# Attention's matrix in the middle of a one-core kernel: VectorE's order fixed, strided sums as trees, and v's products ahead

## The chip, the cores and the metric

The kernel runs on one core of a Trainium2 chip. The metric is the device time of one execution in microseconds (us): the median of three runs before the change is 2695.53 us (2695.43 to 2703.38). A core has a matrix engine (TensorE, here PE), a vector engine (VectorE, DVE), a scalar engine with function tables (ScalarE, ACT), a general engine (GpSimd, POOL) and a queue engine (SyncE, SP). Each takes its own instructions in order and waits on the others through semaphores. DMAs are issued from SP's, ACT's and POOL's queues.

## The reference

The input is `x`, 1 x 384 x 192 x 192, float32. Layer 0 is a preactivated attention over channels, layer 1 a depthwise 7x7 convolution; each is added to its input after a group norm with 32 groups.

```python
qkv = einsum('bchw,oc->bohw', gn(x), w_qkv) + b_qkv      # 1152 channels
qkv = qkv.reshape(b, 3*c, 96, 2, 96, 2).max(axis=(3, 5)) # 2x2 max pool
qkv = depthwise3x3(qkv, w_dw) + b_dw
q, k, v = split(qkv)                                     # 8 heads of 48 channels, 9216 pixels
q, k = q / norm(q), k / norm(k)
attn = einsum('bhcn,bhdn->bhcd', q, k) * temperature     # 8 matrices of 48 x 48
out = sum(topk_softmax(attn, kk) @ v * a for kk, a in zip((24, 32, 36, 38), (a1, a2, a3, a4)))
out = repeat2x2(gelu(out))
x = x + einsum('bchw,oc->bohw', out, w_proj) + b_proj
x = x + depthwise7x7(gn(x), symmetrized(w7))
```

`topk_softmax` keeps the kk largest of the 48 entries of a row and takes the softmax over them.

## The kernel before

The 384 channels lie as three tiles of 128 partitions (`KT = 3`). The kernel has four stages, one after the other on the chip:

1. Statistics of the first group norm, with the weights scaled by them.
2. q and k: products, pooling and nine taps of the depthwise convolution for 24 bands of rows; the squares for the norms; transposes; and `grams`, the 96 x 96 products of pairs of heads, summed in PSUM over all bands (`products`). Towards its end v's first two row blocks are convolved in between (`xvb`).
3. v: a loop over 16 blocks of rows. Block `i` takes part in this way: `load_v(i, t0)` loads a third of it (`t0` = 0, UT, 2 UT) on SP's queue into one of three slots of `xvs`; `convolve(i, t0, ct, ...)` makes six matmuls into a tile of the PSUM pool `pv`, which has **two** buffers, and pools it on VectorE with one reduce (line 569) into the tile `rows`; `depthwise_v(i, ct, dys)` makes three taps on VectorE for each `dy`, into `vb`; `attend(i)` multiplies `vb` by `attnT` (tile `po`) and takes Gelu on ScalarE; `project` multiplies by the projection (tile `pr`, copied out as `y`); `residual` adds `x` on VectorE (tile `sx`), sums squares on ScalarE and stores by POOL's queue. Its four adds per channel tile are counted below as residual adds. Loop turn `i` attends `j = i - 2`, so at its start blocks up to 2 must have been convolved in full.
4. The 7x7 convolution as matmuls (line 1909), with the weights laid out as band matrices.

Between stages 2 and 3 stands the function `attention`, a generator that is advanced in steps (`yield`) while v's products are issued around it. It scales `grams` by the norms of k (`scaled`), gathers the heads' 48 x 48 pieces with ten small DMAs into `att` (128 partitions x 3 x 48), multiplies by q's norms, and then finds each entry's rank in its row by comparing it with all others. The row's two halves of 24 are compared with each other (`sq`, 24 x 24) and within themselves (`tri`, 2 x 24 x 24, cut by the triangle `lower`); sums along both directions of these squares give `seconds`, `firsts`, `before` and `behind`. The rank decides, for each of the four kk, which of the exponentials `ex` stay (`em`); they are normalized, weighted and added to `mix`. `mix` goes by ten small DMAs into the block matrix `diag`, which seven PE transposes (tile `aT`) turn into `attnT`.

Two things set the order on an engine. A tile framework inserts the semaphores that the data need and lets a scheduler choose the order; an instruction passed through `keep` (`tc.keep_in_program_order`) stays in the order in which the program issues it, among those that are kept. Before the change `attention`'s VectorE instructions are not kept: the scheduler mixes them with v's taps and poolings. Attention runs while blocks 2 and the first third of block 3 are convolved, and block 1's taps (for attend(1), the loop's first) are made beside it.

Of the kernel before, what the change touches and what calls it, by code (L numbers as in the profile page):

```python
# [86 lines left out]
def conv_preact_d2(  # L87
# [468 lines left out]
    def convolve(i, t0, ct, xb, pin):  # L556
        b, rows = order[i], place(i)
        o = (2 * KT + ct) * P
        ps = pv.tile([P, UT, 512], F32, name=f"pv{b}_{t0}_{ct}", tag="pv")
        for u in range(UT):  # L560
            for kt in range(KT):
                pin(
                    nc.tensor.matmul(  # L563
                        ps[:, u, 0 : RB * HW], wq[:, kt, o : o + P], xb[:, u, kt, :],
                        start=(kt == 0), stop=(kt == KT - 1),
                    )
                )
        pin(
            nc.vector.tensor_reduce(  # L569
                rows[ct][:, 1 + t0 : 1 + t0 + UT, 1 : PS + 1],  # L570
                ps[:, :, 0 : RB * HW].rearrange("p u (a w b) -> p u w a b", a=2, b=2),
                AX.XY,
                ALU.max,
            )
        )

    with ExitStack() as bx:
# [628 lines left out]
        for _ in products(NB - 1, sides.pop(NB - 1)):  # L1206
            pass
        for args in xvb:
            convolve(*args, pe_keep)
        for tiles in vrows:  # L1210
            row_borders(tiles)
# [3 lines left out]
    def attention(ap):  # L1215

        HH = HC // 2
        lower = ap.tile([P, HH, HH], F32, name="lower")
        nc.gpsimd.memset(lower, 1.0)
        nc.gpsimd.affine_select(  # L1220
            out=lower, in_=lower, compare_op=ALU.is_gt, fill=0.0, base=0,
            pattern=[[1, HH], [-1, HH]], channel_multiplier=0,
        )
# [3 lines left out]
        for i, (mt, r0, r1, h) in enumerate(PIECES):  # L1227
# [3 lines left out]
        scores = nc.vector.tensor_tensor(  # L1231
            att, att, rn[:, 0:KT].unsqueeze(2).to_broadcast([P, KT, HC]), ALU.mult
        )
        yield

        rank = ap.tile([P, KT, HC], F32, name="rank")
        after = ap.tile([P, HH], F32, name="after")
        with tc.issue_after(scores.ins):  # L1240
            nc.vector.tensor_reduce(after, lower.rearrange("p d e -> p e d"), AX.X, ALU.add)
# [3 lines left out]
        for mt in range(KT):  # L1245

            full = [P, HH, HH]
            sq = ap.tile(full, F32, name=f"sq{mt}", tag="sq")
            nc.vector.tensor_tensor(
                sq,  # L1250
                att[:, mt, 0:HH].unsqueeze(1).to_broadcast(full),
                att[:, mt, HH:].unsqueeze(2).to_broadcast(full),
                ALU.is_ge,
            )
            yield
            nc.vector.tensor_reduce(seconds[:, mt], sq, AX.X, ALU.add)
            nc.vector.tensor_reduce(
                firsts[:, mt], sq.rearrange("p d e -> p e d"), AX.X, ALU.add
            )
            yield  # L1260

            full = [P, 2, HH, HH]
            halves = att[:, mt, :].rearrange("p (s d) -> p s d", s=2)
            tri = ap.tile(full, F32, name=f"tri{mt}", tag="tri")
            nc.vector.tensor_tensor(
                tri, halves.unsqueeze(2).to_broadcast(full),
                halves.unsqueeze(3).to_broadcast(full), ALU.is_ge,
            )
            yield
            nc.vector.tensor_tensor(  # L1270
                tri, tri, lower.unsqueeze(1).to_broadcast(full), ALU.mult
            )
            yield
            for t, order in ((before, "p s d e -> p s d e"), (behind, "p s d e -> p s e d")):
                nc.vector.tensor_reduce(
                    t[:, mt].rearrange("p (s d) -> p s d", s=2), tri.rearrange(order), AX.X,
                    ALU.add,
                )
                yield
        nc.vector.tensor_tensor(rank, before, behind, ALU.subtract)  # L1280
        halves = rank.rearrange("p t (s d) -> p (t s) d", s=2)
        nc.vector.tensor_tensor(
            halves, halves, after.unsqueeze(1).to_broadcast([P, 2 * KT, HH]), ALU.add
        )
        nc.vector.tensor_tensor(rank[:, :, HH:], rank[:, :, HH:], seconds, ALU.add)
        nc.vector.scalar_tensor_tensor(
            rank[:, :, 0:HH], rank[:, :, 0:HH], float(HH), firsts, ALU.add, ALU.subtract
# [3 lines left out]
        row3 = [P, KT, HC]  # L1291
        top = ap.tile([P, KT], F32, name="top")
        nc.vector.tensor_reduce(top, att, AX.X, ALU.max)
        ex = ap.tile(row3, F32, name="ex")
        nc.vector.tensor_tensor(ex, att, top.unsqueeze(2).to_broadcast(row3), ALU.subtract)
        nc.scalar.activation(ex, ex, AF.Exp)
        yield
        mix = ap.tile(row3, F32, name="mix")
        for i, kk in enumerate(KKS):
            em = ap.tile(row3, F32, name=f"em{i}", tag="em")  # L1300
            nc.vector.scalar_tensor_tensor(em, rank, float(kk), ex, ALU.is_lt, ALU.mult)
            rs = ap.tile([P, KT], F32, name=f"rs{i}", tag="rs")
            nc.vector.tensor_reduce(rs, em, AX.X, ALU.add)
            nc.vector.reciprocal(rs, rs)
            nc.vector.tensor_scalar_mul(rs, rs, aw[:, i : i + 1])
            rsb = rs.unsqueeze(2).to_broadcast(row3)
            if i == 0:
                nc.vector.tensor_tensor(mix, em, rsb, ALU.mult)
            else:
                nc.vector.tensor_tensor(em, em, rsb, ALU.mult)  # L1310
                nc.vector.tensor_tensor(mix, mix, em, ALU.add)
            yield
        diag = ap.tile([P, KT, C], F32, name="diag")
        nc.gpsimd.memset(diag, 0.0)
        for i, (mt, r0, r1, h) in enumerate(PIECES):
            eng = (nc.gpsimd, nc.scalar)[i % 2]
            eng.dma_start(diag[r0:r1, mt, h * HC : (h + 1) * HC], mix[r0:r1, mt, :])
        yield "last"
        for dt in range(KT):
# [9 lines left out]
            for l, h in ((lo, min(hi, TURN)), (max(lo, TURN), hi)):  # L1329
                if l < h:  # L1330
                    o = (l - TURN) % C
                    nc.vector.tensor_copy(attnT[:, dt, o : o + h - l], ps[:, l:h])
# [23 lines left out]
    vbs, begun = {}, set()  # L1356

    def depthwise_v(i, ct, dys, pin=lambda ins: ins):

        b = order[i % NBC]  # L1360
        if (i, ct) not in vbs:
            tag = f"vlast{i}" if i >= NBC - 1 else "vb"
            vbs[i, ct] = vp.tile(
                [P, NT, PS], F32, name=f"vb{i}_{ct}", tag=tag, bufs=KT if i >= NBC - 1 else 2 * KT
            )
        dst = vbs[i, ct]
        for dy in dys:
            r = b + dy - 1
            t0 = 1 + r // NBC
            rows = place(i + dy - 1)[ct]  # L1370
            for j in range(3):
                src = rows[:, t0 : t0 + NT, j : j + PS]
                w = wd[:, 2 * KT + ct, 3 * dy + j : 3 * dy + j + 1]
                if (i, ct) in begun:
                    pin(nc.vector.scalar_tensor_tensor(dst, src, w, dst, ALU.mult, ALU.add))  # L1375
                else:
                    begun.add((i, ct))
                    pin(
                        nc.vector.tensor_scalar(
                            dst, src, w, bdb[:, 2 * KT + ct : 2 * KT + ct + 1], ALU.mult, ALU.add  # L1380
                        )
                    )


    AHEAD = 3
    with tc.tile_pool(name="ap", bufs=1) as ap:
        chain, seen = attention(ap), []

        def advance(n):
            for _ in range(n):  # L1390
                if "last" not in seen:
                    seen.append(next(chain))

        advance(9)
        i = AHEAD - 1
        for t0 in range(0, NT, UT):
            xb = load_v(i, t0)
            with tc.issue_after(multiplied):
                for ct in range(KT):
                    convolve(i, t0, ct, xb, lambda ins: ins)  # L1400
            advance(6)
        for ct in range(KT):
            depthwise_v(1, ct, (0, 1))

        advance(99)
        xb = load_v(AHEAD, 0)
        for ct in range(KT):
            depthwise_v(AHEAD - 2, ct, (2,), keep)
            convolve(AHEAD, 0, ct, xb, keep)
        for _ in chain:  # L1410
            pass

    bpm = const.tile([P, KT], F32, name="bpm")
    with tc.issue_after(settled):
        nc.vector.tensor_tensor(bpm, bp, mean0, ALU.subtract)
    ysum = const.tile([P, KT, NBC, 2], F32, name="ysum")
# [146 lines left out]
    for i in range(AHEAD, NBC):  # L1563
# [7 lines left out]
        xb = load_v(i, UT)  # L1571
        for ct in range(KT):
            depthwise_v(i - 1, ct, (0, 1), keep)
            if ct == 1:
                convolve(i, UT, 0, xb, keep)
        convolve(i, UT, 1, xb, keep)
        if spare[i - AHEAD]:
            depthwise_v(*spare[i - AHEAD][:2], spare[i - AHEAD][2:], keep)
        convolve(i, UT, 2, xb, keep)
# [425 lines left out]
```

## Time and profile before

| what | value |
|---|---|
| median of three runs | 2695.53 us |
| the profiled execution, and its span | 2711.91 us, 2710.2 us |
| busy: PE, DVE, ACT, POOL | 93%, 84%, 52%, 54% of the span |
| last `grams` matmul ends | 1311.2 us |
| `scaled`, `att` x rn, last `mix` start | 1311.40, 1320.10, 1383.06 us |
| first `po` of attend(1), attend(2), attend(3) | 1392.07, 1443.21, 1492.60 us |
| mean granted clock of PE | 0.982 |

Times are microseconds from the start of the span. In the profile's rows an instruction is named by engine, line, operation and tiles; "[2.08 <-DMA xv]" behind a row is the idle time of that engine before it and what ended it. A row with "x5" merges five instructions in a row, and its time is from the first's start to the last's end. Every fp32 matmul shows as two records. Where engines are put side by side, `(x189)` is a count of instructions, PEclk the granted clock as a share of full speed, and the DMA share the mean of the 16 DMA engines. Waits are given as total us, times, and the longest.

### The profile page before, as it was taken

Reading aid. Unit: us, or ns where it says so; the run is one execution under the profiler, and the core shown is the slowest. Engines: PE = TensorE matmul, PEld = TensorE weight load, DVE = VectorE, ACT = ScalarE, POOL = GpSimd, SP = SyncE. Lnnn points to the kernel's source line nnn. Section 1 sums busy time; section 2 is a strip of 40 time slices with the busy share of each in tenths; the row PEclk is TensorE's granted clock in tenths of the full one; section 3 lists DMA queues with packets and bytes.
Section 4 is the critical chain, followed back from the end, with each engine's and each line's share of the span. In section 5 each row is a group of like instructions: output and inputs, shape, how many; then the busy total and the mean of one; then the engine's idle time right before and its main releaser. Section 6 shows DMA issues by size and latency. Waiting matters only on the chain. (4 is left out here: it accounts for less than half of the span.)

```text
span 2710.2 us, 29562 instructions
## 1 busy us (share of the span) xinstructions
PE 2512.9 (93%) x8893; PEld 1632.4 (60%) x8893; DVE 2268.1 (84%) x3161; ACT 1419.6 (52%) x2710; POOL 1462.8 (54%) x1588
## 2 busy tenths in 40 slices
PE   0298999999999999999889989999999799999998
PEld 0144565656666656555556646666667577777776
DVE  7986788888888888888689969898888789888987
ACT  0032667676767676775112223223225577777776
POOL 1013788888887988875112311001001578787886
PEclk9999999999999999999999989999999899999999
DMA  9962354445453545433429996756747999999998
GB/s 378 394 245 53 117 163 135 137 139 165 131 169 102 175 128 170 128 98 76 136 80 331 372 316 210 250 195 221 239 143 246 331 347 367 371 372 367 372 368 263
DMA packets 467582, 609.59 MB, mean 225 GB/s; under 512 B 250160, under 2 KB 399264, under 8 KB 450656
## 3 DMA queue, kind: packets, MB, share of 16 engines
q1 hardware_dynamic: 406928, 311.80, 36.9%
q0 software_dynamic: 37376, 148.85, 15.4%
q10 hardware_dynamic: 23120, 147.07, 14.4%
q8 instruction: 71, 1.16, 0.2%
q14 instruction: 87, 0.71, 0.1%
HBM read 370.93 MB, written 208.21 MB: 214 GB/s over the span
## 5 line engine op out<-in xcount | busy, mean ns | idle before, releaser
L563 PE MATMUL pv<-xv,wq 128*128 128x384 f32 x1512 | 502.7, 493 | 27.2 <-DMA xv<-in_x_dram 13.5
L1909 PE MATMUL pc<-main,w 128*128 128x288 f32 x1536 | 435.2, 406 | 3.6 <-issue 2.2
L563 PEld LDWEIGHTS pv<-xv,wq 128*128 128x128 f32 x1512 | 290.8, 193 | 230.9 <-DVE rows L569 16.3
L1929 DVE TENSOR_SCALAR apart<-pc,rb 32x576 f32<-32x576 f32 x384 | 312.2, 813 | 75.9 <-PE pc L1909 51.8
L869 POOL TENSOR_TENSOR qk<-qk,more 128x384 f32<-128x384 f32 x290 | 309.6, 1074 | 110.2 <-ACT more L868 101.3
L1927 ACT ACTIVATE apart<-pc,rb 32x576 f32<-32x576 f32 x384 | 281.1, 732 | 133.2 <-PE pc L1909 128.4
L1543 POOL DMA_DIRECT2D sd<-sx x96 | 72.2, 755 | 507.4 <-DVE sx L1502 486.9
L1909 PEld LDWEIGHTS pc<-main,w 128*128 128x128 f32 x1536 | 289.8, 189 | 87.8 <-issue 3.2
L1375 DVE SCALAR_TENSOR_TENSOR vb<-rows,wd,vb 128x576 f32<-128x576 f32 x384 | 312.5, 816 | 10.8
L869 POOL TENSOR_TENSOR qk<-qk,rows 128x384 f32<-128x384 f32 x216 | 230.3, 1070 | 76.3 <-ACT rows L868 70.1
L1909 PE MATMUL pc<-aux,h 128*128 128x288 f32 x768 | 248.5, 406 | 0.5 <-issue 0.3
L901 DVE SCALAR_TENSOR_TENSOR bank_r<-ring,wd,bank_r 128x384 f32<-128x384 f32 x383 | 236.1, 617 | 6.9
L1868 POOL COPY res<-apart 128x1152 f32<-128x1152 f32 (+1 forms) x96 | 224.1, 2360 | 11.1 <-ACT apart L1927 7.3
L1009 PE MATMUL bank_b<-rows,more 128*128 128x384 f32 x528 | 220.4, 499 | 1.9 <-ACT bank_c L1111 0.9
L1502 DVE TENSOR_TENSOR sx<-xr,y 128x576 f32<-128x576 f32 x180 | 203.5, 1172 | 20.7 <-ACT y L1473 14.9
L569 DVE TENSOR_REDUCE rows<-pv 128x192 f32<-128x768 f32 x144 | 137.5, 955 | 69.7 <-PE pv L563 69.6
L1522 ACT ACTIVATE wq<-sx,negmid 128x1152 f32<-128x1152 f32 x96 | 120.6, 1256 | 114.5 <-DVE sx L1502 110.2
L1089 DVE TENSOR_TENSOR rows<-bank_c,rows 128x384 f32<-128x384 f32 x132 | 73.2, 555 | 127.3 <-PE bank_c L1009 69.0
L1752 DVE SCALAR_TENSOR_TENSOR w<-eye,sb,w 128x512 f32<-128x512 f32 x96 | 174.5, 1857 | 1.5
L1909 PEld LDWEIGHTS pc<-aux,h 128*128 128x128 f32 x768 | 144.9, 189 | 42.7 <-POOL main L1817 2.0
L868 ACT ACTIVATE more<-ring,wd 128x384 f32<-128x384 f32 x290 | 170.3, 608 | 0.0
L1009 PE MATMUL bank_x<-xq,wq 128*128 128x384 f32 x378 | 154.7, 491 | 1.0 <-ACT bank_b L1061 1.0
(342 smaller groups left out, 4803.9 us busy)
## 6 DMA issues: line engine op xcount, KB each, us to landing
sd<-sx POOLq DMA_DIRECT2D x96, 600.0 KB, 10.1
out_dram<-res SPq DMA_DIRECT2D x192, 288.0 KB, 10.7
main<-sd ACTq DMA_DIRECT2D x46, 1200.0 KB, 6.3
xr<-in_x_dram SPq DMA_DIRECT2D x45, 1152.0 KB, 12.8
xq<-in_x_dram SPq DMA_DIRECT2D x21, 2304.0 KB, 8.4
xv<-in_x_dram SPq DMA_DIRECT2D x126, 384.0 KB, 7.4
w<-wt ACTq DMA_DIRECT2D x46, 1024.0 KB, 7.5
xs<-in_x_dram SPq DMA_DIRECT2D x24, 1536.0 KB, 15.2
```

Source lines behind the costliest of these rows:

```text
L563: nc.tensor.matmul(ps[:, u, 0 : RB * HW], wq[:, kt, o : o + P], xb[:, u, kt, :], start=(kt == 0), stop=(kt == KT - 1),)
L868: keep(nc.scalar.mul(part.rearrange("p (h w) -> p h w", w=PS), src, w))
L869: keep(nc.gpsimd.tensor_tensor(flat, flat, part, ALU.add))
L901: nc.vector.scalar_tensor_tensor(into, src, w, before, ALU.mult, ALU.add)
L1009: nc.tensor.matmul(ps[:, 0:HN], lhs, rhs, start=start, stop=True, skip_group_check=True)
L1375: pin(nc.vector.scalar_tensor_tensor(dst, src, w, dst, ALU.mult, ALU.add))
L1502: nc.vector.tensor_tensor(bass.AP(flat.tensor, flat.offset + at(e) + a * RUN, [flat.ap[0], [JP, NT], [1, NJ], [at(f) - at(e), 2]],), xq[:, ...
L1752: nc.vector.scalar_tensor_tensor(mid, eye.unsqueeze(1).to_broadcast([P, 4, P]), sb[:, c : c + 1], mid, ALU.mult, ALU.add,)
L1868: keep(copy(res[ps, k], apart[ps, :, k].rearrange("p e n -> p n e")))
L1909: nc.tensor.matmul(ahead[q][:, k, 0 : NT * NJ], lhs, rhs, start=(j == 0), stop=(j == 2), skip_group_check=True,)
L1927: keep(nc.scalar.mul(dst, src, scale))
L1929: keep(nc.vector.tensor_scalar_mul(dst, src, scale))
```

## The change

In words, in the order of the program:

- `depthwise_v` moves up in the file, unchanged. Block 1's first taps, `dy` = 0, for all three channel tiles (nine taps), are issued right after the last `products` and before the last of `xvb`, and those of `dy` = 1 for tile 0 (three taps) after it; all are kept in order. Their sums lie in a tile `vb_early` in the space of the weights' tile `g`.
- In `attention` every VectorE instruction of the chain but `scaled` and `after` is kept. `lower` is made after `att`'s DMAs on POOL, and its sum `after` is issued before the scores.
- The sums along the strided direction, `firsts` and `behind`, are no longer reduces but five adds of halves each (`halved`).
- The top and the exponentials are issued ahead of the rank's sums, followed by a Gelu on one element.
- The four kk's exponentials lie in one array `em`, so that one reduce, one reciprocal and one multiplication serve all four.
- `diag`'s ten DMAs go over three queues, SP's among them, instead of two.
- The middle third of block 3 (`load_v(3, UT)` and its three `convolve`s) moves from loop turn 3, between attend(1) and its `project`, to before attend(1). The seven transposes stand before the last of them. Block 1's other taps of `dy` = 1 and those of `dy` = 2 are each issued in front of one of block 3's six convolutions.

As built, nothing else changes its place but a few instructions of loop turn 3: PE has the transposes between the fifth and sixth convolution of block 3, and `project` directly behind attend(1); VectorE has tile 1's residual adds among block 2's last taps.

```diff
+        early = gwp.tile([P, GR * GQ * TR], F32, name="vb_early", tag="g")
+        for ct in range(KT):
+            vbs[1, ct] = early[:, ct * PBC : (ct + 1) * PBC].rearrange("p (t c) -> p t c", c=PS)
+        for tiles in vrows[0:2]:
+            row_borders(tiles)
+        for ct in range(KT):
+            depthwise_v(1, ct, (0,), keep)
         for args in xvb:
             convolve(*args, pe_keep)
-        for tiles in vrows:
-            row_borders(tiles)
+        depthwise_v(1, 0, (1,), keep)
+        row_borders(vrows[2])
...
-        lower = ap.tile([P, HH, HH], F32, name="lower")
-        nc.gpsimd.memset(lower, 1.0)
...
+        tt = lambda *args: keep(nc.vector.tensor_tensor(*args))
+        total_of = lambda dst, src: keep(nc.vector.tensor_reduce(dst, src, AX.X, ALU.add))
...
+        def halved(dst, t):
+
+            for n in (HH // 2, HH // 4, HH // 8):
+                tt(t[:, :, 0:n], t[:, :, 0:n], t[:, :, n : 2 * n], ALU.add)
+            tt(t[:, :, 0], t[:, :, 0], t[:, :, 1], ALU.add)
+            tt(dst, t[:, :, 0], t[:, :, 2], ALU.add)
...
-            nc.vector.tensor_reduce(seconds[:, mt], sq, AX.X, ALU.add)
-            nc.vector.tensor_reduce(
-                firsts[:, mt], sq.rearrange("p d e -> p e d"), AX.X, ALU.add
-            )
+            total_of(seconds[:, mt], sq)
+            halved(firsts[:, mt].unsqueeze(1), sq.unsqueeze(1))
             yield
...
+            total_of(before[:, mt].rearrange(by_half, s=2), tri)
+            halved(behind[:, mt].rearrange(by_half, s=2), tri)
+            yield
...
+        ready_to = ap.tile([P, 1], F32, name="ready_to")
+        keep(nc.scalar.activation(ready_to, halfneg[:, 0:1], AF.Gelu))
...
+        for i, kk in enumerate(KKS):
+            keep(
+                nc.vector.scalar_tensor_tensor(em[:, i], rank, float(kk), ex, ALU.is_lt, ALU.mult)
+            )
+        total_of(rs.rearrange("p i t -> p (i t)"), em.rearrange("p i t c -> p (i t) c"))
+        keep(nc.vector.reciprocal(rs, rs))
...
-            eng = (nc.gpsimd, nc.scalar)[i % 2]
+            eng = (nc.gpsimd, nc.scalar, nc.sync)[i % 3]
             eng.dma_start(diag[r0:r1, mt, h * HC : (h + 1) * HC], mix[r0:r1, mt, :])
...
+        for t0 in range(0, NT, UT):
+            xb = load_v(i, t0)
+            for ct in range(KT):
+                next(chain)
+                convolve(i, t0, ct, xb, keep)
+        xb = load_v(AHEAD, 0)
+        next(chain)
+        assert next(chain) == "last"
+        for ct in range(KT):
+            if ct > 0:
+                depthwise_v(1, ct, (1,), keep)
+            convolve(AHEAD, 0, ct, xb, keep)
+        xb = load_v(AHEAD, UT)
+        for ct in range(KT):
+            if ct == KT - 1:
+                for _ in chain:
+                    pass
+            depthwise_v(AHEAD - 2, ct, (2,), keep)
+            convolve(AHEAD, UT, ct, xb, keep)
...
-        xb = load_v(i, UT)
+        if i > AHEAD:
+            xb = load_v(i, UT)
         for ct in range(KT):
             depthwise_v(i - 1, ct, (0, 1), keep)
-            if ct == 1:
+            if ct == 1 and i > AHEAD:
                 convolve(i, UT, 0, xb, keep)
```

## The prediction

> **What bounds the kernel now.** I read the engine table and the 40 slices first: PE is busy 93% of the span, at 9 tenths in nearly every slice. The chain that ended last covers only the last 10 us, so it says nothing of the middle. So I looked for the stretch in which the change lives, where PE is not full, with busy time by stretch:
>
> ```profile
> core 0: us, PE busy (x) PEld busy (x) DVE busy (x) ACT busy (x) POOL busy (x), PEclk, DMA share, GB/s
> 1311.20:1392.07 80.87, 64.71 (x189) 36.45 (x188) 72.04 (x103) 5.79 (x22) 9.64 (x15) 0.92 0.43 140
> 1392.07:1443.21 51.14, 51.14 (x168) 33.05 (x169) 41.80 (x59) 15.05 (x31) 15.76 (x17) 0.97 0.52 185
> ...
> 1443.00:1492.00 49.00, 49.00 (x169) 31.71 (x168) 44.65 (x51) 13.77 (x30) 11.87 (x16) 1.00 0.94 317
> ```
>
> The first row is the attention stage: from the end of the last `grams` matmul to the first `po` matmul of attend(1). PE idles 80.87 - 64.71 = 16.2 us, at clock 0.92. The second is block 3 of the loop (attend(2) ends it), the third a later block: both full. After 1443 the loop is PE-bound, with one hole of 13.5 us at 1568-1585 (PE on DMA `xv`), and the last stage is 99% PE again. So I count up to the first matmul of attend(2), 1443.21 in this execution: what moves that moves the end. What PE waits for in the stage, by the waits, then VectorE's timeline:
>
> ```profile
> PE pv L563 <- DVE rows L569: 16.1, 6, 7.2
> ...
> 1311.40 0.55 DVE L1225 TENSOR_TENSOR scaled<-grams,rkb 96x384 f32<-96x384 f32 x1 [2.08 <-DMA xv<-in_x_dram]
> 1315.30 0.96 DVE L569 TENSOR_REDUCE rows<-pv 128x192 f32<-128x768 f32 x1 [3.35 <-PE pv L563]
> 1320.10 0.31 DVE L1231 TENSOR_TENSOR att<-att,rn 128x144 f32<-128x144 f32 x1 [3.84 <-DMA att<-scaled]
> ...
> 1331.48 3.00 DVE L1275 TENSOR_REDUCE behind<-tri 128x48 f32<-128x1152 f32 x1
> 1334.39 1.57 DVE L1257 TENSOR_REDUCE firsts<-sq 128x24 f32<-128x576 f32 x1
> ...
> 1383.06 0.29 DVE L1311 TENSOR_TENSOR mix<-mix,em 128x144 f32<-128x144 f32 x1
> 1383.28 3.72 DVE L1375 SCALAR_TENSOR_TENSOR vb<-rows,wd,vb 128x576 f32<-128x576 f32 x5
> ...
> 1394.53 4.24 DVE L1375 SCALAR_TENSOR_TENSOR vb<-rows,wd,vb 128x576 f32<-128x576 f32 x5
> 1403.73 0.96 DVE L569 TENSOR_REDUCE rows<-pv 128x192 f32<-128x768 f32 x1 [4.96 <-PE pv L563]
> ```
>
> PE waits for VectorE's pooling (L569): `pv` has two buffers, and the reduce that frees one stands in VectorE's queue behind attention's matrix. From 1320 to 1383 VectorE never rests but for 1.45 us. Of PE's own timeline I need these:
>
> ```profile
> 1311.20 11.80 PE L563 MATMUL pv<-xv_begun,wq 128*128 128x384 f32 x36
> 1336.89 22.16 PE L563 MATMUL pv<-xv,wq 128*128 128x384 f32 x60 [4.31 <-DVE rows L569]
> 1383.19 5.72 PE L563 MATMUL pv<-xv,wq 128*128 128x384 f32 x12 [7.21 <-DVE rows L569]
> 1388.75 0.93 PE L1325 MATMUL aT<-ident,diag 128*128 128x128 f32 x7
> 1392.07 7.75 PE L1441 MATMUL po<-vb,attnT 128*128 128x288 f32 x24 [2.39 <-DVE attnT L1332]
> ```
>
> Twelve records are one convolution: 3.92 us at full clock (11.77 for 36, at 1399.65). After a hole of over 2 us PE is slow for a while: 60 records took 22.16 instead of 19.6 (2.5 lost), 12 took 5.72 (1.8), 24 of `po` 7.75 instead of 5.98 (1.8).
>
> **What one link costs on VectorE.** In the five taps at 1383.28 neighbours belong to different sums: (3.72 - 0.81)/4 = 0.73 apart, that is duration less 0.085. In the five at 1394.53 each needs the one before: (4.24 - 0.81)/4 = 0.86, duration plus 0.04. Here a rule speaks. The Trainium skill, "VectorE: DVE Perf Modes", section "The DRAIN you can't avoid", says that the next operation starts only when the pipe has emptied and that a semaphore costs nothing extra. By it, fixing the order costs nothing. By these rows each dependent neighbour costs 0.125 more, and the new order, built, has 99 instructions that wait on VectorE itself between `scaled` and attend(2): 12 us if all were free before, perhaps half of it new, since the scheduler had interleaved sums. I take the rows.
>
> **Part 1, twelve taps in front.** Nine stand between `rkb` (ends 1309.3) and `scaled`: 3 x (0.57 + 2 x 0.81 + links) = 6.7 us or so, so `scaled` ends at 1316.3 instead of 1311.95. 2.1 us of it lies in the wait for `grams`, the rest delays the scores by 4.4. The other three come among the matrix's work. All twelve, about 10 us, leave the end of the stage.
>
> **Part 2, copies and `lower`.** `scaled`'s end to `att` took 8.15 us (1311.95 to 1320.10). POOL's five DMAs now stand before the memset and the select (0.58 and 0.84 us), which held the first back to 1313.80; ACT's five have no fill among them. `scaled` to landing: four issues of 0.61, then 4.3 median, 6.7. Floor 5.9 (five issues of 0.525, memset, select, then the reduce `after`, 1.57); ceiling 8.15. I take 6.7: `att` at 1323.0, 2.9 later than before. The 1.57 of `after` leaves the chain for this wait.
>
> **Part 3, the matrix.** Per third: sq 0.75, seconds 0.75, sq's tree, tri 1.35, times lower 1.35, before 1.35, tri's tree. Tree sizes 288, 24 and 48 have no row; between rows at 72 (0.22), 144 (0.30) and 576 (0.75) elements 288 comes to 0.45, and 24 to 0.17. The same page, on its errata, gives fp32 adds (N + 151)/0.96 ns: 457 and 182. sq's tree: 0.45 + 0.30 + 0.22 + 0.17 + 0.17 = 1.31, with five links 1.51, against 1.57 strided, or 1.49 start to start: **nothing won**. tri's: 0.75 + 0.45 + 0.30 + 0.20 + 0.20 = 1.90, with links 2.10, against 2.91: 0.8 won. A rule speaks against trees, "Rules for kernel authors" of that page: chained operations want fewer instructions, and six reduces become 30 adds. By its 151 cycles each, 24 more cost 3.8 us, more than the 2.4 that I credit; but the sums above hold that fixed part already, so I keep 2.4 (bounds 0 and 4).
> The exponentials: 24 instructions (6.1 us) become 4 x 0.30 + 0.75 + 0.18 + 0.16 + 0.75 + 0.45 + 0.30 = 3.8.
> Durations from `att` to `mix`: 3 x 8.75 = 26.3; `att`, top, ex, rank 1.9; exponentials 3.8; eleven poolings x 0.955 = 10.5; three taps 2.4: 44.9. Links (about 50 x 0.04) and overlaps (about 27 x 0.085) cancel. `mix` is ready at about 1368.2, against 1383.35: 15 us earlier, also because only 3 taps lie inside it instead of some 22.
>
> **Part 4, PE up to attend(1).** Three more convolutions (block 3, UT) come in front: 17, the seven transposes, then one more. 1311.2 + 17 x 3.92 = 1377.8. One hole stays: the fourth convolution needs the second one's reduce, which stands behind `att`, sq, seconds and two adds: 1327, against 1323.0, so about 3.7, plus 1.7 for the slow clock. VectorE then has eleven reduces in 45 us, one per 4.1, so PE runs nearly through. Transposes at 1383.2; `diag` (three queues, SP's behind nine `xv` loads that are released at 1367.6) lands near 1373, hidden by 10 us. Plus 0.93 and 3.92: **attend(1) at 1388.1**, 4.0 earlier. VectorE's 15 taps, 12.8 us, end by 1387.7: both are late together, and whichever I erred on decides.
>
> **Part 5, block 3.** PE has 11.8 us less here: 5.98 + 8.89 + 6 x 3.92 = 38.4 instead of 51.1. But VectorE has 18 taps (14.7), 3 spare taps (2.3), 12 residual adds x 1.14 (13.7), small ones 0.9, 9 taps (7.6), six reduces (5.2): 44.4. `project` now follows attend at once, then two convolutions fill `pv` by 1410.9; the reduce that frees one stands behind 21 taps and 8 adds, at about 1416.5. PE idles 6.5 and loses 1.7 of clock; the convolutions that are left end at 1434.7. **attend(2) at 1434.7 instead of 1443.21: 8.5 us.** The table load of Gelu (row: 1.28 us at 1393.43, next activation 1394.72) was hidden by convolutions, and would now stand before `project`; the dummy Gelu pays it earlier. The skill's "ScalarE: Activation LUTs", "What ACT_TABLE_LOAD costs", adds a drain of 1.38; the row shows none. 1.3 or 2.7 us are kept off, none gained against before.
>
> Without the two clock losses the same sum gives 1431.6, 11.6 us. The clock loss after the second hole may be less, so I take **9.5 us: 2695.5 - 9.5 = 2686**. The sum is made on the profiled execution (2711.9 us, span 2710.2); the median is 0.6% shorter, which changes 9.5 us by nothing.
>
> **What may collide.** From 1470 to 1600 the DMA share is 1.03, and PE's hole at 1568 is its debt. The burst starts with block 4's residual, 21.2 us behind attend(2), and share 0.59 at 1460-1470 shows the burst before it drained. The new first residual comes at about 1402 (before 1415.06), the next at 1456: 54 apart against 49. The hole moves with the loop.
>
> **Rivals.**
> - Forecast, 0.50: 2686, own range 2682 to 2690 (gains of 13.5 to 5.5).
> - More, 0.26: PE regains its clock at once, `att` lands at the floor, links overlap. Links at -0.085 instead of +0.04 bring attend(2) to 1427: 16 us, 2679.5. For it: small holes (0.54, 0.80) cost no clock. Against: every hole over 2 us did.
> - Given back in block 3, 0.15: `att` at the ceiling and 2.5 lost per hole give 1437.8, 5.4 us: 2690; with block 3's 12 us given back wholly, 4: 2691.5. For it: DMA share 0.88 at 1311-1320.
> - Slower, 0.09: the links. If a held instruction costs 0.16 rather than 0.04, attend(2) is at 1443.9, no gain; from there each 0.1 is 10 us, so at 0.25 the time is 2705. Only rows of 576 elements and [128 x 6] (1299.85, 1300.05) show a link; 30 new ones are of 24 to 288 elements. Against: both sizes show 0.03 to 0.04.
>
> A measurement tells 0.3%, 8.1 us, from none; the forecast lies just beyond. Faster: 0.7 of the forecast (its range from 8.1 us up) and the second case, 0.35 + 0.26 = 0.61. Same: the rest of it and the third case, 0.30. Slower 0.09. The range, 2677 to 2697, reaches past the second case and to the point where the links begin to cost.
>
> **What would show it.** `scaled` near 1316 and `att` near 1323 (part 1, 2); `mix` near 1368 (3); `behind`'s six instructions near 2.1 us together; a PE hole of 3 to 5 us near 1323 and one of 5 to 8 near 1411; first `po` matmuls near 1388 and 1435. Wrong if `mix` comes after 1375, or if no hole shows in block 3.

## The result and the profile after

| | before | after |
|---|---|---|
| median, nine runs each | 2695.96 us | 2689.47 us |
| ratio, 95% interval | | 0.9970 (0.9958 to 0.9983) |
| medians of a second comparison (22 and 17 runs) | 2697.10 us | 2688.31 us |
| its ratio, 95% interval | | 0.9967 (0.9957 to 0.9977) |
| profiled execution and its span | 2711.91, 2710.2 us | 2689.47, 2687.8 us |

The kernel is 6.5 to 8.8 us faster, where 9.5 were forecast. The two profiled executions differ by 22.4 us, far more than the medians; the first experiment explains that. Busy time by stretch, of the kernel after: the first row goes from the end of the last `grams` matmul to attend(1), the second on to attend(2).

```profile
core 0: us, PE busy (x) PEld busy (x) DVE busy (x) ACT busy (x) POOL busy (x), PEclk, DMA share, GB/s
1312.10:1390.82 78.72, 73.62 (x226) 43.10 (x224) 68.65 (x111) 7.26 (x24) 7.13 (x12) 0.96 0.43 140
1390.82:1437.13 46.31, 40.07 (x133) 25.99 (x132) 43.32 (x60) 14.11 (x30) 17.83 (x18) 0.93 0.57 207
```

Before, these stretches took 80.87 and 51.14 us. So attend(2) comes 125.0 us behind `grams` instead of 132.0. PE's work moved from the second stretch to the first (64.71 to 73.62 busy, 51.14 to 40.07), and the second now has idle time. PE's timeline of the kernel after shows where it idles:

```profile
1312.10 11.80 PE L563 MATMUL pv<-xv_begun,wq 128*128 128x384 f32 x36
1329.00 57.35 PE L563 MATMUL pv<-xv,wq 128*128 128x384 f32 x168 [5.09 <-ACT rows L534]
1386.18 0.93 PE L1364 MATMUL aT<-ident,diag 128*128 128x128 f32 x7
1386.95 4.04 PE L563 MATMUL pv<-xv,wq 128*128 128x384 f32 x12
1390.82 5.98 PE L1449 MATMUL po<-vb_early,attnT 128*128 128x288 f32 x24
1396.64 8.89 PE L1473 MATMUL pr<-gl,wp 128*128 128x288 f32 x36
1405.37 7.90 PE L563 MATMUL pv<-xv,wq 128*128 128x384 f32 x24
1419.51 17.79 PE L563 MATMUL pv<-xv,wq 128*128 128x384 f32 x48 [6.24 <-DVE rows L569]
1437.13 5.98 PE L1449 MATMUL po<-vb,attnT 128*128 128x288 f32 x24
```

Two holes (stretches in which PE waits) are left, 5.09 and 6.24 us, and behind each PE is slow for a while: 168 records took 57.35 instead of 14 x 3.92 = 54.9, and 48 took 17.79 instead of 15.7. Seven transposes, 24 convolutions, attend(1) and `project` are 0.93 + 94.1 + 5.98 + 8.89 = **109.9 us of PE's own work** between `grams` and attend(2), in both kernels. Before: 16.2 of holes and 6.1 of lost clock on top; after: 11.3 and 4.5. (Rows that follow each other overlap a little, so these sums come out 0.2 and 0.7 us above 132.0 and 125.0.)

VectorE's timeline of the kernel after, in part:

```profile
1317.57 0.55 DVE L1256 TENSOR_TENSOR scaled<-grams,rkb 96x384 f32<-96x384 f32 x1
1318.04 0.94 DVE L569 TENSOR_REDUCE rows<-pv 128x192 f32<-128x768 f32 x1
1322.57 1.58 DVE L1269 TENSOR_REDUCE after<-lower 128x24 f32<-128x576 f32 x1 [3.59 <-POOL lower L1264]
1325.30 0.31 DVE L1253 TENSOR_TENSOR att<-att,rn 128x144 f32<-128x144 f32 x1 [1.16 <-DMA att<-scaled]
1325.64 0.76 DVE L1253 TENSOR_TENSOR sq<-att 128x576 f32<-128x576 f32 x1
1326.43 0.75 DVE L1254 TENSOR_REDUCE seconds<-sq 128x24 f32<-128x576 f32 x1
1327.22 0.80 DVE L1253 TENSOR_TENSOR sq<-sq 128x288 f32<-128x288 f32 x2
1327.94 0.95 DVE L569 TENSOR_REDUCE rows<-pv 128x192 f32<-128x768 f32 x1
...
1338.32 1.84 DVE L1253 TENSOR_TENSOR tri<-tri 128x576 f32<-128x576 f32 x4
1340.19 0.21 DVE L1253 TENSOR_TENSOR behind<-tri 128x48 f32<-128x48 f32 x1
...
1371.43 0.31 DVE L1253 TENSOR_TENSOR mix<-em 128x144 f32<-128x144 f32 x1
...
1415.01 2.17 DVE L1510 TENSOR_TENSOR sx<-xr,y 128x576 f32<-128x576 f32 x2
1417.21 1.16 DVE L1510 TENSOR_TENSOR sx<-xr,y 128x576 f32<-128x576 f32 x1
1418.51 0.95 DVE L569 TENSOR_REDUCE rows<-pv 128x192 f32<-128x768 f32 x1
```

`mix` is done 11.6 us earlier than before (1371.74 against 1383.06 + 0.29), or 12.5 counted from the end of `grams`: before, 23 of VectorE's taps ran between `att` and `mix`, now three do. But it no longer decides: its DMAs, then the transposes at 1386.18, have time to spare. Three experiments below (k8, k9, k12) bring it 4 to 7 us earlier still, and attend(1) comes no sooner. The pooling of 1327.94 is the one that PE's first hole waits for (it ends at 1328.89, PE goes on at 1329.00). The profile names ScalarE's `rows` there, which ended 0.45 us before that pooling did. The second hole ends with the pooling of 1418.51 (it ends at 1419.46, PE goes on at 1419.51), which stands behind eight residual adds, the last three of them in the two rows above it. One thing runs otherwise than the description of the change has it: the order of kept instructions is not quite the program's. Tile 0's three taps, issued ahead of the scores, run behind `tri` times `lower`.

### The profile page after: what moved, and what is told of

Read it like the earlier page. It is cut to its first block, busy times and chain, and to the rows that moved or that the text cites. A ratio compares the mean times of both kernels' runs of the same rounds, so it can differ in the third digit from the quotient of the medians.

```text
span 2687.8 us, 29574 instructions
## 1 busy us (share of the span) xinstructions
PE 2509.0 (93%) x8893; PEld 1628.8 (61%) x8893; DVE 2270.1 (84%) x3172; ACT 1420.9 (53%) x2711; POOL 1462.9 (54%) x1587
## 3 DMA queue, kind: packets, MB, share of 16 engines
q8 instruction: 71, 1.16, 0.2%
## 5 line engine op out<-in xcount | busy, mean ns | idle before, releaser
L897 POOL TENSOR_TENSOR qk<-qk,more 128x384 f32<-128x384 f32 x290 | 309.7, 1074 | 109.9 <-ACT more L896 100.9
L1551 POOL DMA_DIRECT2D sd<-sx x96 | 72.4, 757 | 493.0 <-DVE sx L1510 474.4
L596 DVE SCALAR_TENSOR_TENSOR vb<-rows,wd,vb 128x576 f32<-128x576 f32 x360 | 293.8, 818 | 10.7
L897 POOL TENSOR_TENSOR qk<-qk,rows 128x384 f32<-128x384 f32 x216 | 230.5, 1072 | 76.2 <-ACT rows L896 69.9
L1456 ACT ACTIVATE gl<-po 128x288 f32<-128x288 f32 x96 | 39.5, 411 | 225.2 <-PE po L1449 225.2
```

Of the source, the lines that this page charges most:

```text
L897: keep(nc.gpsimd.tensor_tensor(flat, flat, part, ALU.add))
```

## The experiments

All times in the table are us from the end of `grams` in a profiled execution of that kernel, taken as the start of the first `pv` row behind it; a difference under 2 us tells little, as the two rows of the unchanged kernels show.

| kernel | `att` | `mix` | attend(1) | attend(2) |
|---|---|---|---|---|
| before, first and k1 | 8.9, 8.9 | 71.9, 72.4 | 80.9, 81.4 | 132.0, 131.1 |
| after, first and k11 | 13.2, 12.7 | 59.3, 57.6 | 78.7, 77.0 | 125.0, 123.0 |
| k2, `scaled` first | 9.0 | 53.5 | 71.8 | 118.8 |
| k3, pooling ahead of `att` | 12.8 | 55.9 | 74.2 | 120.5 |
| k4, no products ahead | 13.2 | 59.3 | 72.8 | 124.5 |
| k5, strided sums | 12.8 | 59.5 | 77.8 | 123.5 |
| k6, pooling ahead of adds | 12.0 | 56.9 | 76.2 | 119.0 |
| k7, no early Gelu | 12.7 | 57.6 | 76.9 | 123.0 |
| k8, order free | 12.7 | 52.3 | 78.1 | 124.2 |
| k9, no early taps | 8.8 | 52.2 | 78.1 | 123.2 |
| k12, k9 and k5 | 8.7 | 53.8 | 79.6 | 124.5 |
| k10, three moves | 8.9 | 53.4 | 71.7 | 113.3 |

**The two unchanged kernels again (k1, k11).**

> The kernel before, unchanged, profiled once more. In the two profiled executions the changed kernel is 22.4 us shorter in its span, but the medians differ by 6.5. Theory A: only the stretch up to attend(2) is the change's (132.0 us from the end of grams before, 125.0 after), and the 13.5 us in which PE waits for xv near 1568 vary from execution to execution. Then this profile shows 132 +- 1.5 up to attend(2) again, but another total of PE's waits for xv (0 to 20 us), and the span moves with it. Rival B: the hole near 1568 belongs to the old order, and the change took it away. Then it is here again, 13 +- 1 us at the same place, and the span is 2708 to 2712.

> The changed kernel, unchanged, once more, for its median beside the other kernels of this call and for its spread. Theory A (att's copies and the clock behind the first hole vary from execution to execution, which alone parts 76.2, 76.9 and 78.7 us for attend(1) in three kernels of one order): attend(1) at 76 to 79 us behind grams, attend(2) at 122.5 to 125.5; the median 5 to 9 us below before. Rival B (78.7 belongs to this kernel): 78.7 +- 0.3 and 125.0 +- 0.3 again.

PE's waits behind 1440 us, of the first profile of before and of k1 (us in total, times, the longest):

```profile
PE pv L563 <- DMA xv<-in_x_dram: 13.5, 3, 7.9
```

```profile
PE pv L563 <- DMA xv<-in_x_dram: 1.7, 2, 1.0
```

The hole is not the kernel's: theory A. From attend(2) to the end of the span the first profile of before took 1267.0 us, and all the 13 others, of every kernel here, took 1246.8 to 1255.3. So the 16 us or so that the first two profiles differ by there are that one execution. k11 (theory A there too) shows that the stage varies as well: 123.0 against 125.0, from `att`'s copies (0.5) and the clock behind the first hole (56.11 against 57.35 us for the same 168 records). Compared with k1 the stage is 6 to 8 us shorter, as the medians are.

**Where the holes come from (k2, k3, k6).** k2:

```diff
         for ct in range(KT):
             vbs[1, ct] = early[:, ct * PBC : (ct + 1) * PBC].rearrange("p (t c) -> p t c", c=PS)
+        scaled = early[:, KT * PBC : KT * PBC + C]
+        keep(nc.vector.tensor_tensor(scaled[0:PAIR], grams[0:PAIR], rkb[0:PAIR], ALU.mult))
```

> Only `scaled` is moved: it stands ahead of the nine early taps, so that the copies of att run beside them. Theory A (VectorE's queue decides att, the first hole and attend(1)): `scaled` ends at the end of grams + 0.6 us instead of + 6.0; att 3 to 5 us earlier, the hole of 5.1 us shrinks to 0 to 2, mix 3 to 4.5 earlier; attend(1) 2 to 5 earlier and attend(2) 2 to 4 earlier than in the changed kernel (78.7 and 125.0 us from the end of grams): the time about 3 us shorter. Rival B (the copies wait for busy DMA queues, not for `scaled`): att stays within 1 us of its place, 13.2 us behind grams, and nothing moves.

VectorE's timeline of k2 (`scaled` now lies in the tile `vb_early`), and PE's first hole:

```profile
1311.51 0.55 DVE L1240 TENSOR_TENSOR vb_early<-grams,rkb 96x384 f32<-96x384 f32 x1 [2.06 <-PE grams L796]
...
1318.00 1.57 DVE L1269 TENSOR_REDUCE after<-lower 128x24 f32<-128x576 f32 x1
1319.49 0.81 DVE L596 SCALAR_TENSOR_TENSOR vb_early<-rows,wd,vb_early 128x576 f32<-128x576 f32 x1
1320.33 0.31 DVE L1255 TENSOR_TENSOR att<-att,rn 128x144 f32<-128x144 f32 x1
```

```profile
1322.95 7.90 PE L563 MATMUL pv<-xv,wq 128*128 128x384 f32 x24
1331.53 47.12 PE L563 MATMUL pv<-xv,wq 128*128 128x384 f32 x144 [0.68 <-DVE rows L569]
```

The taps now run while the copies are under way (no idle time stands before `att`). `att` comes 3.7 to 4.2 us earlier, the hole shrinks to 0.68 with no clock lost behind it (144 records in 47.12), and attend(1) at 71.8 is PE's own work, 18 x 3.92 + 0.93 = 71.5. The gain is more than expected: 5 to 7 us at attend(1) where 2 to 5 were, 4 to 6 at attend(2) where 2 to 4 were. One more thing moved with it: the pooling that the hole waits for ran right behind `att` (at 1321.29), ahead of `sq`, instead of behind four of the matrix's instructions. In its old place it would have ended some 12.6 us behind `grams`, about 1 us after PE needs it (an estimate from the rows of both kernels), so most of the 5 us of the hole is still `att`'s earlier start. Time: 2682.59 us, 0.9951 of before (0.9936 to 0.9966).

k3 moves one multiplication:

```diff
-        for args in xvb:
-            convolve(*args, pe_keep)
+        pooled_v = [convolve(*args, pe_keep) for args in xvb]
...
-        tt(att, att, rn[:, 0:KT].unsqueeze(2).to_broadcast([P, KT, HC]), ALU.mult)
+        with tc.issue_after(pooled_v[1].ins):
+            tt(att, att, rn[:, 0:KT].unsqueeze(2).to_broadcast([P, KT, HC]), ALU.mult)
```

> Only one instruction is moved: the multiplication of att by rn, and with it the matrix behind it, stands behind the pooling of the third convolution of the stage instead of ahead of it. Theory A (the first hole of PE is the pooling behind the matrix in VectorE's queue): the hole of 5.1 us near 1324 goes to below 1, its clock loss of 2.4 with it; attend(1) 2 to 5 us earlier than 78.7 us behind grams, attend(2) 1 to 4 earlier than 125.0. Rival B (the hole is ScalarE's: the trace names its fill of a rows tile as the last releaser): the hole stays at 4 to 5 us. Rival C (VectorE alone decides attend(1), PE's hole is free): the hole goes, but attend(1) stays within 1 us.

PE's timeline of k3:

```profile
1324.73 8.07 PE L563 MATMUL pv<-xv,wq 128*128 128x384 f32 x24 [1.21 <-ACT rows L534]
1334.35 47.13 PE L563 MATMUL pv<-xv,wq 128*128 128x384 f32 x144 [1.54 <-DVE rows L569]
```

Two small holes, 1.21 and 1.54 us (one below 1 was expected), took the place of the large one, and next to no clock was lost (24 records in 8.07, 144 in 47.13). So the hole was the pooling behind the matrix, not ScalarE. attend(1) comes 3 to 4.5 us earlier, and the time is 0.9960 of before (0.9946 to 0.9975).

k6 does the same in block 3:

```diff
         for ot in range(2):
+            if ot == 1 and i == AHEAD:
+                convolve(i, 2 * UT, 0, xb, keep)
             for _ in sums[ot]:
                 pass
-        convolve(i, 2 * UT, 0, xb, keep)
+        if i > AHEAD:
+            convolve(i, 2 * UT, 0, xb, keep)
```

> In loop turn 3 the first convolution of block 3's last third is issued behind the first channel tile's residual adds instead of behind the second's, so that its pooling stands four adds earlier in VectorE's queue; all else of the change stays. Theory A (block 3's hole is that pooling, behind four adds of 1.14 us): the hole of 6.2 us becomes 1.5 to 2.5, attend(1) stays at 78.7 us behind grams, attend(2) comes 3 to 5 us earlier than 125.0, the time 3 to 4 us shorter. Rival B (VectorE's own work between attend(1) and attend(2) is the bound): the hole is cut up, but PE waits for other poolings instead, and attend(2) stays within 1 us.

PE's timeline of k6:

```profile
1413.49 17.45 PE L563 MATMUL pv<-xv,wq 128*128 128x384 f32 x48 [2.98 <-DVE rows L569]
```

The hole went from 6.24 to 2.98 us (1.5 to 2.5 were expected), attend(1) to attend(2) from 46.3 (46.0 in k11) to 42.7: theory A, 3.3 to 3.6 us for four adds' place in a queue. attend(1) comes a little sooner in k6 too, but it lies ahead of the edit and is not its doing.

**The parts undone (k4, k5, k7, k8, k9, k12).** k4 puts block 3's middle third back behind attend(1).

```diff
-        xb = load_v(AHEAD, UT)
...
-            convolve(AHEAD, UT, ct, xb, keep)
...
-        if i > AHEAD:
-            xb = load_v(i, UT)
+        xb = load_v(i, UT)
```

> Block 3's middle third is put back behind attend(1), between it and project, as before; all else of the change stays. Theory A (v's products ahead move PE's work but not the end of the stage, since block 3 becomes VectorE's): attend(1) 4 to 10 us earlier than in the changed kernel (69 to 75 us behind grams), attend(1) to attend(2) 51 to 53 us instead of 46.3 and without the hole of 6.2; attend(2) at 121 to 127 behind grams, so within 3 us of the changed kernel. Rival B (these products are where the gain is, since PE idles before attend(1) without them): attend(1) within 3 us of 78.7, attend(2) at 129 to 132, the time 4 to 7 us longer, about as before the change.

PE's timeline of k4:

```profile
1384.82 8.36 PE L1447 MATMUL po<-vb_early,attnT 128*128 128x288 f32 x24 [5.53 <-DVE attnT L1371]
```

attend(1) came 4 to 6 us earlier, now waiting for VectorE's `attnT`; the way from it to attend(2) took 51.75 us, and attend(2) stayed, at 124.5: theory A. The time is 0.9974 of before (0.9957 to 0.9991), not to be told from the changed kernel's.

k5 puts back the strided reduces:

```diff
         def halved(dst, t):
-            for n in (HH // 2, HH // 4, HH // 8):
-                tt(t[:, :, 0:n], t[:, :, 0:n], t[:, :, n : 2 * n], ALU.add)
-            tt(t[:, :, 0], t[:, :, 0], t[:, :, 1], ALU.add)
-            tt(dst, t[:, :, 0], t[:, :, 2], ALU.add)
+            total_of(dst, t.rearrange("p s d e -> p s e d"))
```

> The five adds of halves are put back to one strided reduce each (firsts and behind), kept in order; all else of the change stays. Theory A (the prediction's sum): each reduce along tri's strided direction costs 2.9 to 3.0 us instead of the tree's 2.08, one along sq's 1.5 instead of 1.5, so att to mix takes 48.8 us instead of 46.4; attend(1) and attend(2) 0 to 2.5 us later, since VectorE has hardly an idle us left there. Rival B (each add costs its fixed part, 0.157 us, on top, so 24 more instructions cost 3.8): att to mix is shorter without trees, 45 to 46. Rival C (the tree saves VectorE time, and PE alone decides attend(1)): att to mix 48 to 49, attend(1) within 0.5 of 78.7 us behind grams.

`att` to `mix` took 46.7 us, against 46.1 (with 1.63 us of waits for PE inside) and 44.9 (0.47 inside) in the changed kernel: 2.2 or 2.3 us more without the waits, and nothing at attend(1). The trees do save VectorE about what was worked out (2.4); here it buys nothing (rival C for the end; its 48 to 49 left out that the waits shrink).

k7 leaves out the Gelu on one element.

> Left out is the Gelu on one element ahead of attend(1), which loads the function table early. Theory A (the prediction's: the load then stands ahead of project, with no convolutions in between to hide it): project starts 1.3 us later (2.7 with a drain), with a hole in PE of that size. Rival B: the six matmul groups of attend(1) take 5.98 us, and the half that project needs first is through Gelu 2 us before project starts, so the load of 1.28 us is hidden; project starts within 0.3 us, and nothing moves.

ScalarE's timeline of k7:

```profile
1388.76 1.28 ACT L1454 ACT_TABLE_LOAD   x1 [26.17 <-DVE rows L569]
1390.06 1.01 ACT L1454 ACTIVATE gl<-po 128x288 f32<-128x288 f32 x3
```

The load takes 1.28 us; the three Gelus that `project` needs first end at 1391.07, and `project` starts at 1393.53, right behind attend(1)'s matmuls, 6.05 us behind the first of them against 5.82 in k11. Rival B: hidden but for 0.2 us.

k8 lets the scheduler order the matrix (the two helpers and the other `keep`s of `attention` on VectorE are gone):

```diff
-        tt = lambda *args: keep(nc.vector.tensor_tensor(*args))
-        total_of = lambda dst, src: keep(nc.vector.tensor_reduce(dst, src, AX.X, ALU.add))
+        tt = lambda *args: nc.vector.tensor_tensor(*args)
+        total_of = lambda dst, src: nc.vector.tensor_reduce(dst, src, AX.X, ALU.add)
```

> Attention's VectorE instructions are not kept in order: the scheduler mixes the thirds' squares, triangles and tops, so that of the neighbours between att and mix some 35 more do not depend on one another; all else of the change stays. Theory A (a dependent neighbour costs 0.125 us more): att to mix shorter by 2 to 4 us than 46.4, but the pooling behind att comes one square later, the first hole grows from 5.1 to about 6, and attend(1) and attend(2) stay within 1 us of 78.7 and 125.0 us behind grams. Rival B (the fixed order is what brings the change's gain): mix 3 us or more later, attend(2) 3 or more later. Rival C (links are nothing): att to mix within 1 us of 46.4.

VectorE's timeline of k8, where `sq` and `tri` now alternate:

```profile
1325.18 0.76 DVE L1253 TENSOR_TENSOR sq<-att 128x576 f32<-128x576 f32 x1
1325.86 1.35 DVE L1253 TENSOR_TENSOR tri<-att 128x1152 f32<-128x1152 f32 x1
1327.13 0.74 DVE L1254 TENSOR_REDUCE seconds<-sq 128x24 f32<-128x576 f32 x1
1327.79 0.95 DVE L569 TENSOR_REDUCE rows<-pv 128x192 f32<-128x768 f32 x1
...
1364.44 0.31 DVE L1253 TENSOR_TENSOR mix<-em 128x144 f32<-128x144 f32 x1
```

`att` to `mix` took 39.6 instead of 46.1 us. One pooling fewer stands inside (0.9) and no wait for PE (1.6); 4.0 are left for some 35 neighbours that no longer depend on each other, 0.11 us each. The rows show it: `tri` starts 0.08 before `sq` ends, where in the fixed order `seconds` starts 0.03 behind `sq` (1325.64 + 0.76, then 1326.43). Yet attend(1) and attend(2) did not move, and the first hole stayed as well (4.91 us, where about 6 was expected). The fixed order costs VectorE 4 us, off the path.

k9 sets the twelve early taps behind `mix` (`depthwise_v(1, ct, (0, 1), keep)` ahead of block 3's first three convolutions), and k12 puts k5's strided reduces into that.

> Part 1 undone: block 1's twelve early taps stand behind mix, with its other fifteen, instead of ahead of `scaled` and among the matrix's instructions; all else of the change stays. Theory A (VectorE's sum up to attend(1) is the bound, and twelve taps that save nothing but the wait for grams and part of the wait for att's copies): att 7.5 to 8.5 us behind grams instead of 12 to 13, mix at 51 to 54 instead of 57 to 59, but 27 taps and six poolings then stand in front of attend(1): it comes at 77 to 81 us, within 2 of the changed kernel's 76.2 to 78.7, and the hole near 1324 is gone. Rival B (the twelve taps in front are the gain): attend(1) at 84 or later, attend(2) at 130 or later, as before the change. Rival C (only PE's 18 convolutions and its holes decide): with the hole gone attend(1) comes at 72 to 74.

> Two parts undone together that cost next to nothing alone: the twelve early taps stand behind mix, and the five adds of halves are strided reduces again. Theory A (undone singly, each is paid out of VectorE's slack, which there is only once; without the early taps VectorE is the bound up to attend(1), 78.1 us): the trees' 2.4 us now show in full, attend(1) at 80 to 81.5 us behind grams and attend(2) at 125 to 127, against 77.0 and 123.0 with both. Rival B (these two parts are worth nothing, together too, and the gain lies elsewhere): attend(1) at 77.5 to 79, attend(2) within 1 us of 123.2.

k9: the first hole is gone, but two others (2.69 and 1.49 us) stand near 1369 and 1380, where the 27 taps hold the poolings; attend(1) at 78.1, as theory A has it. Placed in front of `scaled`, as the change does, the taps are worth nothing; behind it (k2) they bring attend(2) 4.4 us earlier than without them (k9). k12, with the early taps and the trees both undone, lies between its expectations: 1.5 us later at attend(1), 1.3 at attend(2), not 2.4. Part of the trees' gain still fell into waits.

**The moves together (k10):** k2 and k6, and the spare taps of turn 3 given to turn 4 (`spare = [()] + [...]`).

> The moves that helped, together: `scaled` ahead of the nine early taps, the first convolution of block 3's last third behind one tile's residual adds instead of two, and the three spare taps of loop turn 3 given to turn 4. Theory A (PE's own work from grams to attend(2) is 109.9 us, and all above it is holes and the clock lost behind them): both holes shrink to below 1.5, attend(1) at 71.5 to 73 us behind grams, attend(2) at 112 to 116 instead of 125.0, the time 9 to 12 us below the changed kernel's, 2677 to 2680. Rival B (VectorE becomes the bound in block 3, and the taps that are put off come back in turn 4): attend(2) at 116 to 119, and what is gained up to there beyond 7 us is lost by attend(3).

Busy time by stretch of k10, to attend(1) and to attend(2):

```profile
1311.10:1382.80 71.70, 71.04 (x225) 41.37 (x224) 68.94 (x112) 7.27 (x24) 7.10 (x12) 1.00 0.48 155
1382.80:1424.39 41.59, 38.31 (x134) 24.96 (x133) 40.73 (x57) 14.10 (x30) 17.10 (x17) 1.00 0.51 181
```

Holes of 0.56, 2.12 and 1.16 us are left (the last two in block 3, over the 1.5 that A allowed for one), and the clock stays at 1.00: 113.3 us instead of 123.0 to 125.0, of which 109.9 is PE's work. What the spare taps' move adds by itself was not tried. The gain is not lost later: attend(3) comes at 162.7 us, against 174.4 in the first profile after and 172.4 in k11. **2679.16 us, 0.9929 of before (0.9915 to 0.9944), 9.15 us below the changed kernel's median in the same comparison**: the best version here.

## Why the prediction held

- **The bound** was read rightly: PE waits for poolings that stand behind the matrix, and what moves attend(2) moves the end. k2, k3, k6 and k10 moved attend(2), and the time followed (in k6, one execution; the others have four to six).
- **The sum**, from `grams` to attend(1) and attend(2), was 76.9 and 123.5 us; measured 78.7 and 125.0 in one execution, 77.0 and 123.0 in another. 8.5 us was the sum; the 9.5 that was named rested on the second hole costing less clock. It did not: 2.1 and 1.8 us lost, where 1.7 was put in. The 8.5 should have stood. That the sum is met to 0.5 us in k11 is in part luck: there a hole 0.9 us too long and a clock loss 0.5 too small nearly make up for each other.
- **Terms off in size.** `scaled` came 6.0 us behind `grams`, not 5.1: in k11 one of the nine taps was held up by 0.9 (below), in the first profile `rkb` was ready 0.6 later and a tap was held up by 0.2. `scaled` to `att`: 7.2 and 6.7, for 6.7. The first hole: 5.1 and 4.6, for 3.7, and its clock 2.4 and 1.2, for 1.7. `att` to the end of `mix`: 46.4 and 45.2, for 45.2 (the durations listed add to 44.9). The terms named for part 2's floor add to 5.6, not 5.9; `after` ended 6.0 behind `scaled`. attend(1) to attend(2): 46.3 and 46.0, for 46.6, the hole 6.24 in both, for 6.5.
- **A tri tree** at 2.10 us was measured at 2.08 (1338.32 to 1340.40). The rule against more instructions, weighed there, would have cost VectorE time; k5 sides with the rows.
- **Links.** 0.125 us a link was right (0.11 in k8), and by the two statements quoted from the skill (no extra cost for a semaphore, the next operation waits for the drain) k8 should have gained nothing on VectorE. The same section adds that an operation which is not held starts earlier; with that the rows agree (`tri` 0.08 us before the end of `sq`). The rival "Slower: the links" fell all the same: short instructions pay 0.03 to 0.04 like long ones, and the cost lies where VectorE has slack.
- **Wrong: the table load.** "Would now stand before `project`": attend(1)'s own 5.98 us of matmuls hide it (k7).
- **Wrong: the DMA hole** "moves with the loop". It is one execution's, and the base of 2711.9 us with it.
- **Not seen: that the parts take the place of each other.** Each of the parts that were undone alone leaves attend(2) at 123 to 124.5 us. Without v's products ahead (k4), a shorter VectorE queue brings attend(1) to 72.8, and attend(2) comes at 124.5. With them but without early taps and trees (k12), attend(2) comes at 124.5 as well. Holes and lost clock together are some 15.5 us in both, 15.8 in the changed kernel and 22.3 before, so nearly the whole gain stays either way. Which part brings it is therefore open. The trees and the early taps are not needed for it, nor for the earlier `mix`: k12 has it at 53.8 us, against 71.9 before. What the taps' place behind `mix`, one array of exponentials, or `after` in the wait for the copies is worth alone was not tried, nor v's products undone together with another part.

## What to carry to other kernels

Between two engines that feed each other through two buffers, look for the one instruction that frees a buffer and count what stands ahead of it in its queue: moving four adds or one multiplication behind it was worth 3 to 4 us here; making the arithmetic elsewhere 2 to 4 us shorter or longer (k5, k8) moved nothing. Start a chain of small DMAs before the work that can fill its wait, not behind it. A part undone alone shows only what it adds to the others: here no single part, and not the one pair tried, moved attend(2) by more than 1.5 us, and all together are worth 6 to 8.

## What the runs showed of the hardware

A tap that starts a sum (line 600, one tensor and two scalars per partition) usually takes 0.57 us, but took longer in several places where GpSimd was filling a tile. POOL's timeline and VectorE's, of k11, then of the kernel after:

```profile
1310.96 1.06 POOL L1353 MEMSET diag<- 128x1152 f32 x1 [11.65 <-DMA xv<-in_x_dram]
```

```profile
1310.83 1.50 DVE L600 TENSOR_SCALAR vb_early<-rows,wd,bdb 128x576 f32<-128x576 f32 x1
```

```profile
1397.00 6.60 POOL L1434 MEMSET sx<- 128x2504 f32 x3 [22.95 <-PE po L1449]
```

```profile
1401.41 2.50 DVE L600 TENSOR_SCALAR vb<-rows,wd,bdb 128x576 f32<-128x576 f32 x1
```

The tap ends 0.31 us behind the fill each time (1312.33 behind 1312.02; 1403.91 behind 1403.60), and so in k2 and k3 beside `diag`'s fill (0.97 and 1.20 us, ends 0.30 and 0.31 behind it). The Trainium skill, "SBUF — State Buffer", section "SBUF: two separate sides", says that GpSimd and some VectorE operations share a pair of ports as an exclusive lock, and that the one that comes second waits for the whole instruction. The rows agree in that the tap waits until the fill is over. They do not in which came first: in k11 the tap's record starts 0.13 us ahead of the fill's. A tap with a longer lead, 0.35 us ahead of the fills of `sx` in the kernel after (1396.65 against 1397.00), kept its 0.57 us. The wait cost 0.2 to 0.9 us ahead of `scaled` and 1.9 us in block 3, ahead of the pooling that PE's second hole waits for. Moving the fills was not tried.

PE's clock after a hole was the other surprise. The same 168 records lost 2.4 us behind a hole of 5.1 (after) and 1.2 behind one of 4.6 (k11). The granted clock (PEclk) in the first and the second 5 us behind that hole, of the kernel after and then of k11:

```profile
1329.00:1334.00 5.00, 5.00 (x8) 2.82 (x9) 4.86 (x8) 0.00 (x0) 0.00 (x0) 0.50 1.07 378
1334.00:1339.00 5.00, 5.00 (x15) 2.83 (x14) 4.29 (x5) 0.00 (x0) 0.00 (x0) 0.91 0.32 111
```

```profile
1327.11:1332.11 5.00, 5.00 (x11) 2.70 (x12) 4.86 (x8) 0.00 (x0) 0.00 (x0) 0.66 1.07 380
1332.11:1337.11 5.00, 5.00 (x17) 3.01 (x16) 4.86 (x7) 0.00 (x0) 0.00 (x0) 1.00 0.42 147
```

The prediction's "every hole over 2 us" does not hold. Behind 2.12 us (k10, block 3) and 2.13 us (k1, ahead of attend(1)) the granted clock was 1.00; behind 2.39 us (before, the same place as in k1) and 2.69 us (k9) it was 0.66 over the next 5 us; behind one of 3.01 us late in k5 (at 2064.74) it was 1.00 again. So the length of a hole alone does not tell the loss. What does was not tried.
